# Routed FFN's weights in runs of 2 KB, two weight tiles in other buffers, and the output bias as a row of the projection

## The chip, the cores and the metric

The kernel runs on one core of a Trainium2 chip (trn2). The metric is the device time of one execution in microseconds, median of several runs. A profile is one execution more, with its own time.

## The reference, cut to what matters

For four sequences of 512 tokens with 256 features:

```python
x = x + attn(cond(x, cond_8))          # attention output projection: ... @ Wo.T + bo
x = x + ffn(cond2(x, cond_8))          # routed FFN of 8 experts, 1024 wide
# ffn: 8 groups of 256 tokens; softmax router, two experts per token, at most 128 rows
# per expert and group
expert_in = jnp.einsum('gth,gtec->gech', xg, dispatch)
h = jax.nn.gelu(jnp.einsum('gech,ehf->gecf', expert_in, wi))
expert_out = jnp.einsum('gecf,efh->gech', h, wo)
out = jnp.einsum('gech,gtec->gth', expert_out, combine)
```

`cond` is a gated FFN with weights chosen per sequence, `cond2` a linear layer whose weights are mixed per sequence. Everything is float32. `attn` has 16 heads of 16 with one shared key and value head.

## The kernel before

**Attention stage** (to about 478 us). The attention of the four sequences runs as 64 steps of a loop written out by hand, 16 steps for each sequence. Each step has score matmuls with their maxima (`maxima`), the same scores with exponentials (`exponentials`), and the product with the values (`weigh`). Beside each step, a table (`beside`, `last`) puts pieces of work of the sequences before and after it: `queries`, `keys`, `values` of the next one, and normalising, output projection (`out0` to `out3`, line 442), mixing (`mix0`, `mix1`), routing and scattering of the earlier ones. [...]

The output projection multiplies `attn` (128 rows: four heads of 32 rows, of which 16 are used) by `wo_sb`. Row 16 of each head holds the softmax sum, so after normalising it is one; the projection's matrix has zeros there. The result has the input x added (line 447) into `r`, which is stored as rows of the output by SP (line 448). The input for this sum is loaded by `residual(b)` (lines 290 to 295): SP loads x in 512 KB into a buffer of one copy, and POOL adds the output bias `bo_sb` to it (line 294). `residual` is called for sequences 0, 1 and 2 at steps 17, 33 and 49 and for sequence 3 after the loop.

**Routing.** A token's features, number, expert and two probabilities form a row of 260 floats. POOL scatters each sequence's rows with eight indirect DMAs (`send`, line 604) into `xp` in HBM, sorted by expert.

**Routed FFN.** The rows are worked on in 39 tiles of 128 rows of one expert (`NTILE`). For a tile t:

- `fetch_in(t)` reads the expert from a table into a register of SP and loads `wi`, 1 MB, 8 KB in one run for each of 128 partitions (line 803);
- `fetch_rows(t)` loads the tile's 128 rows from `xp` (line 815); that of tile 0 and that of tile 5 wait for all scatters issued so far;
- `fetch_out(t)` loads `wo`, 1 MB in the same way (line 824);
- `turn(t)` transposes the rows on PE (line 830), DVE copies the result to SBUF (`xT`, line 832);
- `up(t)` is 32 matmuls (line 849), with the gelu on ACT (line 853);
- `put(t)` is 16 matmuls (line 865), and on DVE a few small instructions for weights (`w0`, `w1`) and row numbers (`at`, four buffers) and the weighting into `y` (line 883). POOL then adds `y` to the output's rows with an accumulating indirect DMA (line 884).

Each accumulating DMA, an add in short, waits for the one before it, since they may meet in the same rows. `wi` and `wo` have three buffers each in the pool `wexp`, `y` has two.

The first five tiles are early ones (`NEARLY`): they are full of rows before the last sequence is routed. `table_of_early`, at step 62, issues `wi` of tiles 0 to 2, the rows of tiles 0 to 4 and `wo` of tiles 0 to 2. The halves of `up` of the early tiles are put between the last sequence's pieces by the list `final`. `table_of_rest` then computes the table of the other 34 tiles, and this follows:

```python
for t in range(NEARLY, NEARLY + 3):
    fetch_in(t)
for t in range(NEARLY):
    put(t)
    if t + 3 < NEARLY:
        fetch_out(t + 3)
```

After it, the loop over the other 34 tiles has `up(t)`, `fetch_in(t + 3)`, `fetch_rows(t + 3)`, `turn(t + 1)`, `put(t - 1)` and `fetch_out(t + 2)` in this order.

All plain loads and stores stand in one queue, SP's; scatters and adds stand in POOL's.

Of the kernel before, what the change touches and what calls it, by code (L numbers as in the profile page):

```python
# [9 lines left out]
F32 = mybir.dt.float32  # L10
I32 = mybir.dt.int32
AF = mybir.ActivationFunctionType
ALU = mybir.AluOpType
# [3 lines left out]
P = 128  # L17
B = 4
T = 512
NT = B * T  # L20
D = 256
NE = 8
HC = 512
NH = 16
HD = 16
F = 1024
# [5 lines left out]
NTILE = 2 * NCH + NE - 1  # L32
NEARLY = 5
# [5 lines left out]
def adaln_attn_ffn_kernel(  # L39
# [10 lines left out]
    wv: bass.AP,  # L50
    bv: bass.AP,
    wo: bass.AP,
    bo: bass.AP,
    xtok: bass.AP,
    w2: bass.AP,
    mask2: bass.AP,
# [6 lines left out]
    nc = tc.nc  # L63
# [3 lines left out]
    wexp = ctx.enter_context(tc.tile_pool(name="wexp", bufs=3))  # L67
# [47 lines left out]
    qp = attn_ctx.enter_context(tc.tile_pool(name="qp", bufs=2))  # L115
# [29 lines left out]
    def load(ap, shape, name):  # L145
        t = const.tile(shape, F32, name=name)
        nc.sync.dma_start(t, ap)
        return t
# [5 lines left out]
    wv_sb = load(wv, [P, 2, 32], "wv_sb")  # L154
    bv_sb = load(bv[0:1, :].to_broadcast([P, 32]), [P, 32], "bv_sb")
    wo_sb = load(wo, [P, 4, D], "wo_sb")
    bo_sb = load(bo[0:1, :].to_broadcast([P, D]), [P, D], "bo_sb")
    bias2_sb = load(bias2[0:1, :].to_broadcast([P, D]), [P, D], "bias2_sb")
    wr_sb = load(wr, [P, 2, NE], "wr_sb")

# [129 lines left out]
    def residual(b):  # L290

        t = rp.tile([P, 4, D], F32, name="x", bufs=1)
        nc.sync.dma_start(t, xtok[:, ts(b, 4), :])
        nc.gpsimd.tensor_tensor(t, t, bo_sb.unsqueeze(1).to_broadcast([P, 4, D]), ALU.add)
        seqs[b]["x"] = t

    def project(b):
# [444 lines left out]
    def experts_of_tiles(t0, n, end, step, start):  # L742


        past = fp.tile([P, n, NE], F32, name=f"past{t0}", bufs=1)
        nc.vector.tensor_tensor(
            past, tilen[:, 0:n].unsqueeze(2).to_broadcast([P, n, NE]),
            end.unsqueeze(1).to_broadcast([P, n, NE]), ALU.is_ge,
        )
        te = texp[:, t0 : t0 + n]  # L750
        nc.vector.tensor_reduce(te, past, AX.X, ALU.add)
        nc.vector.tensor_scalar(
            table[:, 1, t0 : t0 + n], te, float(NE - 1), float(P), ALU.min, ALU.mult
        )
        nc.vector.tensor_tensor(past, past, step.unsqueeze(1).to_broadcast([P, n, NE]), ALU.mult)
        row = fp.tile([P, n], F32, name=f"trow{t0}", bufs=1)
        nc.vector.tensor_reduce(row, past, AX.X, ALU.add)
        if start is not None:
            nc.vector.tensor_scalar(row, row, start, None, ALU.add)
        nc.vector.tensor_tensor(row, row, tilen[:, 0:n], ALU.add)  # L760
        nc.vector.tensor_scalar(
            table[:, 0, t0 : t0 + n], row, float(NE * NG), float(P), ALU.min, ALU.mult
        )

    def table_of_early():
        tiles_of_experts(full, -float(P), ALU.is_ge)
        end = ends_of_experts(full, "end0")
        step = fp.tile([P, NE], F32, name="step0", bufs=1)
        nc.vector.tensor_scalar(step, full, -1.0, float(NG), ALU.mult, ALU.add)
        experts_of_tiles(0, NEARLY, end, step, None)  # L770

        nc.vector.tensor_tensor(used[:, 0:NE], full, end, ALU.subtract)
        nc.vector.tensor_scalar(
            used[:, 0:NE], used[:, 0:NE], float(NEARLY), 0.0, ALU.add, ALU.max
        )
        nc.vector.tensor_tensor(used[:, 0:NE], used[:, 0:NE], full, ALU.min)
        for t in range(3):
            fetch_in(t)
        for t in range(NEARLY):
            fetch_rows(t)  # L780
        for t in range(3):
            fetch_out(t)

    def table_of_rest():
        tiles = fp.tile([P, NE], F32, name="tiles", bufs=1)
# [10 lines left out]
    reg, adds, spare = {}, [], {}  # L796
    AFTER = mybir.DependencyInfo(mybir.DependencyClass.Sync, mybir.DependencyReason.DATA)

    def fetch_in(t):

        reg[t] = nc.sync.value_load(table[0:1, 1, t : t + 1], min_val=0, max_val=(NE - 1) * P)
        wi_of[t] = wexp.tile([P, 2, F], F32, name="wi_sb")
        nc.sync.dma_start(wi_of[t].rearrange("p c f -> p (c f)"), wi[ds(reg[t], P), :])

    def fetch_rows(t):

# [13 lines left out]
            tc.add_to_no_dep_group("early tiles", i.ins)  # L820

    def fetch_out(t):
        wo_of[t] = wexp.tile([P, F // P, D], F32, name="wo2_sb")
        nc.sync.dma_start(wo_of[t].rearrange("p c f -> p (c f)"), wo2[ds(reg.pop(t), P), :])

    def turn(t):

# [30 lines left out]
    def put(t, halves=(0, 1)):  # L858

        if halves[0] == 0:  # L860
            po_of[t] = bank("e")
        po = po_of[t]
        for half in halves:
            for fc in range(4 * half, 4 * half + 4):
                mm(  # L865
                    po[:, 0:D], hT_of[t][:, fc, :], wo_of[t][:, fc, :],
                    start=fc == 0, stop=fc == F // P - 1,
                )
        if halves[-1] == 0:
            return  # L870
        xt = xt_of[t]
        number, e0, p0, p1 = (xt[:, D + k : D + k + 1] for k in range(4))
        te = texp[:, t : t + 1]
        w0 = fp.tile([P, 1], F32, name="w0")
        nc.vector.tensor_scalar(w0, e0, te, p0, ALU.is_equal, ALU.mult)  # L875
        w1 = fp.tile([P, 1], F32, name="w1")
        nc.vector.tensor_scalar(w1, e0, te, p1, ALU.not_equal, ALU.mult)  # L877
        nc.vector.tensor_tensor(w0, w0, w1, ALU.add)
        nc.vector.tensor_scalar(w1, number, 0.0, spare1, ALU.is_equal, ALU.mult)
        at = fp.tile([P, 1], I32, name="at", bufs=4)  # L880
        nc.vector.scalar_tensor_tensor(at, number, -1.0, w1, ALU.add, ALU.add)
        y = fp.tile([P, D], F32, name="y")
        nc.vector.tensor_scalar(y, po[:, 0:D], w0, None, ALU.mult)  # L883
        i = nc.gpsimd.indirect_dma_start(  # L884
            out=out_rows,
            out_offset=bass.IndirectOffsetOnAxis(ap=at, axis=0),
            in_=y,
            in_offset=None,
            compute_op=ALU.add,
        )  # L890

        if t > 0:
            tc.add_manual_dep(i.ins, adds[-1].ins.name, AFTER, reason="same rows")
        if t < NEARLY:
            tc.declare_no_dep(i.ins, group="last rows", reason="other sequences")
            tc.add_to_no_dep_group("early adds", i.ins)
        if t == NEARLY:
            for k in last_rows:
                tc.add_manual_dep(i.ins, k.ins.name, AFTER, reason="rows of the last sequence")
        adds.append(i)  # L900

    for n in range(STEPS + 1):
        m = n + LEAD
        if n % 16 == 1 and n > 1:
            residual(n // 16 - 1)
        if m < STEPS:
            maxima(m, (0, 1))
            exponentials(n, (2, 3))
        elif n < STEPS:
            exponentials(n, (0, 1, 2, 3))  # L910
        if n > 0:
            weigh(n - 1)
        if m < STEPS:
            maxima(m, (2, 3))
            exponentials(n, (0, 1))
        if m <= STEPS + 1 and m % 4 == 1:
            shifted(m // 4 - 1)
        if n < STEPS:
            side(*divmod(n, 16))
    work[B - 1] = finish(B - 1)  # L920
    residual(B - 1)
    def half_up(t, half):
        if half == 0:
            turn(t)
# [16 lines left out]
        fetch_in(t)  # L941
    for t in range(NEARLY):
        put(t)
        if t + 3 < NEARLY:
            fetch_out(t + 3)
        if t == 2:
            for k in range(NEARLY, NEARLY + 3):
                fetch_rows(k)
            fetch_out(NEARLY)
        if t == 3:  # L950
            fetch_out(NEARLY + 1)
    turn(NEARLY)
    for t in range(NEARLY, NTILE + 1):
        if t < NTILE:
            up(t, (0, 1))
            if t + 3 < NTILE:
                fetch_in(t + 3)
                fetch_rows(t + 3)
            if t + 1 < NTILE:
                turn(t + 1)  # L960
        if t > NEARLY:
            put(t - 1)
        if t + 2 < NTILE:
            fetch_out(t + 2)


def _layouts(i):
# [3 lines left out]
    def halves(w):  # L971

        *lead, k, n = w.shape
        return np.swapaxes(w.reshape(*lead, k // P, P, n), -3, -2)

    i = {name: np.asarray(a) for name, a in i.items()}
    f32 = np.float32
# [19 lines left out]
    bv = np.ones((1, 32), f32)  # L997
    bv[0, :HD] = bkv[HD:]
    wo = np.zeros((4, 32, 4, D), f32)
    wo[:, :HD] = i["L0_attn_Wo"].T.reshape(4, 4, HD, D).transpose(1, 2, 0, 3)  # L1000
    bias2 = i["L0_cond2_bias"]
    return {
# [8 lines left out]
        "wv": wv,  # L1011
        "bv": bv,
        "wo": wo.reshape(P, 4, D),
        "bo": i["L0_attn_bo"].reshape(1, D),
        "xtok": i["x"].reshape(NCH, P, D).transpose(1, 0, 2),
        "w2": halves(np.swapaxes(i["L0_cond2_weight"], 1, 2)).transpose(1, 0, 2, 3),
        "mask2": halves(i["L0_cond2_mask"].T),
        "bias2": bias2.reshape(1, D),
        "wr": halves(i["L0_ffn_w_router"]),
        "wi": halves(i["L0_ffn_wi"]).reshape(NE * P, 2 * F),  # L1020
        "wo2": halves(i["L0_ffn_wo"]).reshape(NE * P, F * D // P),
    }


# [21 lines left out]
```

## Time and profile before

| | |
|---|---|
| runs (us) | 836.52, 837.17, 837.45; median 837.17 |
| profiled execution | 838.61 us, span from first to last instruction 836.9 |
| busy in the span | PE 768.9 us (92%), PE weight loads 483.6, DVE 351.0, ACT 246.8, POOL 126.8 |
| DMA | 122.21 MB, 146 GB/s on the mean |
| mean granted PE clock | 0.959 |

The span counts from the first to the last instruction; the execution's own time is 1.7 us longer. A line of the timeline or of the groups names the engine (PE matmul, PEld weight load, DVE, ACT, POOL; SPq is SP's queue of DMA issues), the line of the kernel, the operation, and the tiles written and read. Buffer numbers are left out of names, so `wo_sb` is both the attention's projection and the FFN's second weights, `x` both the input and the rows to be scattered. The brackets at the end of a timeline row say how long the engine stood idle before it and what ended that.

### The profile page before, as it was taken

The numbers are of one execution on the slowest core, as the hardware profiler recorded it, in microseconds if no ns is written. First come the engines' busy times: TensorE is split into PE (matmuls) and PEld (weight loads), VectorE is DVE, ScalarE is ACT, GpSimd is POOL, SyncE is SP. The second block draws the span as 40 slices with busy tenths as digits, with TensorE's granted clock in tenths as the row PEclk, the third lists the DMA queues.
The fourth block names the chain that finished last, engine by engine and source line by source line (L and its number), as shares of the span: only waits on it lengthen the run. The fifth ranks groups of instructions, "written<-read, shape, count | busy, mean of one in ns | idle before, by whom it ended". The sixth has DMA issues, their size and how long they took to land. (4 is left out here: it accounts for less than half of the span.)

```text
span 836.9 us, 11311 instructions
## 1 busy us (share of the span) xinstructions
PE 768.9 (92%) x4382; PEld 483.6 (58%) x4382; DVE 351.0 (42%) x826; ACT 246.8 (29%) x419; POOL 126.8 (15%) x128
## 2 busy tenths in 40 slices
PE   2999999999999999999899777948999999999994
PEld 1443433333345434545254266837999989999994
DVE  0165454556655567646875431431222222212221
ACT  0112206554643555434335510301111111111110
POOL 6400010000000010120103301042211212212222
PEclk9999999999999999989899959978999999999998
DMA  8993000000000100020001273196999999999972
GB/s 311 317 296 79 1 25 1 1 1 1 0 1 20 33 0 1 15 88 1 1 14 64 81 287 118 51 339 185 361 304 339 316 320 319 330 296 344 318 239 25
DMA packets 40389, 122.21 MB, mean 146 GB/s; under 512 B 4624, under 2 KB 25360, under 8 KB 29840
## 3 DMA queue, kind: packets, MB, share of 16 engines
q1 hardware_dynamic: 32032, 105.81, 36.3%
q0 software_dynamic: 8304, 15.69, 7.6%
q8 instruction: 34, 0.56, 0.3%
q14 instruction: 19, 0.16, 0.1%
HBM read 101.36 MB, written 20.12 MB: 145 GB/s over the span
## 5 line engine op out<-in xcount | busy, mean ns | idle before, releaser
L353 DVE TENSOR_REDUCE negm<-ps_m 128x1 f32<-128x512 f32 x250 | 160.7, 686 | 103.6 <-PE ps_e L379 95.3
L380 ACT ACTIVATE e<-ps_e 128x512 f32<-128x512 f32 x244 | 132.6, 595 | 152.4 <-PE ps_e L379 141.4
L379 PE MATMUL ps_e<-qs,k 32*128 32x512 f32 x488 | 158.1, 656 | 1.8 <-DVE sm L516 0.9
L849 PE MATMUL ps_m<-xT,wi_sb 128*128 128x128 f32 x1248 | 150.4, 279 | 8.9 <-DVE xT L832 8.3
L349 PE MATMUL ps_m<-k,q 32*128 32x512 f32 x500 | 153.5, 652 | 2.8 <-DVE negm L353 2.7
L849 PEld LDWEIGHTS ps_m<-xT,wi_sb 128*128 128x128 f32 x1248 | 147.9, 195 | 13.8 <-DVE xT L832 11.5
L865 PE MATMUL ps_e<-wo_sb,hT 128*128 128x256 f32 x560 | 126.5, 379 | 0.0
L853 ACT ACTIVATE hT<-ps_m 128x512 f32<-128x512 f32 x70 | 41.8, 597 | 241.6 <-PE ps_m L849 226.8
L865 PEld LDWEIGHTS ps_e<-wo_sb,hT 128*128 128x128 f32 x560 | 103.8, 190 | 12.7
L349 PEld LDWEIGHTS ps_m<-k,q 32*128 32x128 f32 x500 | 42.8, 186 | 87.8 <-DVE negm L353 44.8
L884 POOL DMA_INDIRECT out_dram<-y,at x39 | 60.5, 1551 | 216.0 <-DVE y L883 185.5
L883 DVE TENSOR_SCALAR y<-ps_e,w 128x256 f32<-128x256 f32 x39 | 18.9, 484 | 169.7 <-DMA out_dram<-y,at 146.0
L391 PE MATMUL ps_a<-e,v 128*32 128x512 f32 x512 | 69.8, 618 | 1.1 <-ACT e L380 1.1
L379 PEld LDWEIGHTS ps_e<-qs,k 32*128 32x128 f32 x488 | 52.1, 186 | 10.8 <-ACT e L380 10.2
L604 POOL DMA_INDIRECT xp<-x,to_i x32 | 31.6, 987 | 103.6 <-issue 47.3
L260 PE MATMUL ps_a<-xT_sb,wi_sb 128*128 128x512 f32 x64 | 32.3, 629 | 15.7 <-DMA wi_sb<-in_wcond_dram,rows 15.7
L536 POOL TENSOR_SCALAR x<-mk 128x4 f32<-128x4 f32 x4 | 0.8, 198 | 261.9 <-DVE mk L533 261.9
L391 PEld LDWEIGHTS ps_a<-e,v 128*32 128x32 f32 x512 | 10.2, 109 | 51.7 <-issue 47.3
L307 PE MATMUL ps_c<-coT,wq_sb 128*128 128x512 f32 x64 | 34.5, 671 | 2.0 <-ACT q L308 2.0
L442 PE MATMUL ps_c<-wo_sb,attn 128*128 128x256 f32 x128 | 31.9, 402 | 4.1 <-DVE r L447 4.1
L832 DVE COPY xT<-ps_a 128x256 f32<-128x256 f32 x39 | 16.3, 417 | 44.5 <-PE ps_a L830 44.5
L265 DVE SCALAR_TENSOR_TENSOR hid<-ps_e,wo_sb,sg 128x512 f32<-128x512 f32 x16 | 12.0, 750 | 51.5 <-PE ps_e L262 50.2
(155 smaller groups left out, 631.7 us busy)
## 6 DMA issues: line engine op xcount, KB each, us to landing
wi_sb<-in_wi_dram SPq DMA_DIRECT2D x39, 1024.0 KB
wo_sb<-in_wo_dram SPq DMA_DIRECT2D x39, 1024.0 KB
xp<-zeros SPq DMA_DIRECT2D x1, 8450.0 KB
xt<-xp SPq DMA_DIRECT2D x34, 130.0 KB
xT_sb<-in_xT_dram SPq DMA_DIRECT2D x4, 512.0 KB
w_sb<-in_w_dram SPq DMA_DIRECT2D x8, 256.0 KB
x<-in_xtok_dram SPq DMA_DIRECT2D x4, 512.0 KB
out_dram<-r SPq DMA_DIRECT2D x16, 128.0 KB
```

The costliest lines, as they stand in the source:

```text
L260: mm(pu, wu[:, c, ts(hc, P)], xT_sb[:, c, ts(b, T)], start=c == 0, stop=c == 1)
L307: mm(pq, wq_sb[:, c, i, :], coT[:, c, ts(b, T)], start=c == 0, stop=c == 1)
L349: mm(pm, q[32 * j : 32 * j + 32, ds((4 * hg + hh) * P, P)], k[32 * j : 32 * j + 32, :], start=True, stop=True,)
L353: nc.vector.tensor_reduce(nm[:, hh, j, HD : HD + 1], pm, AX.X, ALU.max, negate=True)
L379: mm(px, k[rows_j, ts(sc, P)], qs_of[u][rows_j, :], start=True, stop=True)
L380: nc.scalar.activation(e_of[n][:, :, j, :], px.rearrange("p (h n) -> p h n", h=4), AF.Exp)
L391: mm(pa_of[u][32 * hh : 32 * hh + 32, :], seqs[b]["v"][:, sc, :], e[:, hh].rearrange("p j n -> p (j n)"), start=sc == 0, stop=sc == 3,)
L442: mm(px[:, 0:D], s["attn"][:, hg, ts(ch, P)], wo_sb[:, hg, :], start=hg == 0, stop=hg == 3,)
L849: mm(ph[:, ts(n, P)], wi_of[t][:, c, ts(4 * half + n, P)], xT_of[t][:, c, :], start=c == 0, stop=c == 1,)
L853: nc.scalar.activation(hT_of[t][:, ds(4 * half, 4), :].rearrange("p f t -> p (f t)"), ph, AF.Gelu_apprx_tanh,)
L865: mm(po[:, 0:D], hT_of[t][:, fc, :], wo_of[t][:, fc, :], start=fc == 0, stop=fc == F // P - 1,)
L884: i = nc.gpsimd.indirect_dma_start(out=out_rows, out_offset=bass.IndirectOffsetOnAxis(ap=at, axis=0), in_=y, in_offset=None, compute_op=AL ...
```

## The change

Four things change.

1. **Runs of 2 KB.** `wi` and `wo` of each expert lie in HBM as four blocks of 256 KB, each with 2 KB for every partition, so a tile's load has four runs of 2 KB for each partition instead of one of 8 KB. The SBUF side is as before.
2. **Buffers.** `wo` of tile 3 goes into a buffer of the pool that holds the queries (`q`), `wo` of tile 4 into one that holds attention output (`o`), both of 8 KB for each partition and out of use by then. Both are issued in `table_of_early`. In the loop over `put` of the early tiles, `wo` of tiles 5 and 6 is then issued before the rows of tiles 5 to 7, and `wo` of tile 7 after them. `y` of tiles 0 to 3 lies in the place of the buffer `rT`; from tile 4 on `y` has three buffers.
3. **Bias.** The output bias is the projection matrix's row 16 of the first head, where the attention has its one. The load of `bo_sb` and POOL's additions are gone.
4. **x** is loaded at steps 0, 28, 44 and 57.

```diff
@@ residual
         t = rp.tile([P, 4, D], F32, name="x", bufs=1)
         nc.sync.dma_start(t, xtok[:, ts(b, 4), :])
-        nc.gpsimd.tensor_tensor(t, t, bo_sb.unsqueeze(1).to_broadcast([P, 4, D]), ALU.add)
@@ experts_of_tiles
-            table[:, 1, t0 : t0 + n], te, float(NE - 1), float(P), ALU.min, ALU.mult
+            table[:, 1, t0 : t0 + n], te, float(NE - 1), 4.0 * P, ALU.min, ALU.mult
@@ table_of_early
         for t in range(3):
             fetch_out(t)
+        for t in range(3, NEARLY):
+            expert_of(t)
+            fetch_out(t)
@@
+    def expert_of(t):
+        reg[t] = nc.sync.value_load(table[0:1, 1, t : t + 1], min_val=0, max_val=(NE - 1) * 4 * P)
+
+    def quarters(w, src, row):
+        nc.sync.dma_start(
+            w.rearrange("p a b -> p (a b)").rearrange("p (q n) -> p q n", q=4),
+            src[ds(row, 4 * P), :].rearrange("(q p) n -> p q n", p=P),
+        )
+
     def fetch_in(t):
-        reg[t] = nc.sync.value_load(table[0:1, 1, t : t + 1], min_val=0, max_val=(NE - 1) * P)
+        if t not in reg:
+            expert_of(t)
         wi_of[t] = wexp.tile([P, 2, F], F32, name="wi_sb")
-        nc.sync.dma_start(wi_of[t].rearrange("p c f -> p (c f)"), wi[ds(reg[t], P), :])
+        quarters(wi_of[t], wi, reg[t])
     def fetch_out(t):
-        wo_of[t] = wexp.tile([P, F // P, D], F32, name="wo2_sb")
-        nc.sync.dma_start(wo_of[t].rearrange("p c f -> p (c f)"), wo2[ds(reg.pop(t), P), :])
+        if t == NEARLY - 2:
+            w = qp.tile([P, T, 4], F32, name="q").rearrange("p (f a) i -> p f (a i)", f=F // P)
+        elif t == NEARLY - 1:
+            w = ep.tile([P, 4, 512], F32, name="o").rearrange("p g (a d) -> p (g a) d", a=2)
+        else:
+            w = wexp.tile([P, F // P, D], F32, name="wo2_sb")
+        quarters(w, wo2, reg[t])
+        wo_of[t] = w
@@ put
-        y = fp.tile([P, D], F32, name="y")
+        if t < 4:
+            if t == 0:
+                spare["y"] = rp.tile([P, 2, T], F32, name="rT", bufs=1).rearrange(
+                    "p a (b d) -> p (a b) d", d=D
+                )
+            y = spare["y"][:, t, :]
+        else:
+            y = fp.tile([P, D], F32, name="y", bufs=3)
@@ the steps
-        if n % 16 == 1 and n > 1:
-            residual(n // 16 - 1)
+        if n in (0, 28, 44, 57):
+            residual((0, 28, 44, 57).index(n))
@@
     work[B - 1] = finish(B - 1)
-    residual(B - 1)
@@ the early tiles
     for t in range(NEARLY):
         put(t)
-        if t + 3 < NEARLY:
-            fetch_out(t + 3)
-        if t == 2:
+        if t < 3:
+            fetch_out(NEARLY + t)
+        if t == 1:
             for k in range(NEARLY, NEARLY + 3):
                 fetch_rows(k)
-            fetch_out(NEARLY)
-        if t == 3:
-            fetch_out(NEARLY + 1)
@@ the other tiles
-        if t + 2 < NTILE:
+        if NEARLY + 3 <= t + 2 < NTILE:
             fetch_out(t + 2)
@@ layouts on the host
+    def quarters(w):
+        return np.swapaxes(halves(w).reshape(NE, P, 4, 512), 1, 2).reshape(-1, 512)
...
+    wo[0, HD, 0] = i["L0_attn_bo"]
...
-        "wi": halves(i["L0_ffn_wi"]).reshape(NE * P, 2 * F),
-        "wo2": halves(i["L0_ffn_wo"]).reshape(NE * P, F * D // P),
+        "wi": quarters(i["L0_ffn_wi"]),
+        "wo2": quarters(i["L0_ffn_wo"]),
```

More of the change, by code (lines that the diff above doesn't have):

```diff
@@ L52, in adaln_attn_ffn_kernel @@
     wo: bass.AP,
-    bo: bass.AP,
     xtok: bass.AP,
@@ L156, in adaln_attn_ffn_kernel @@
     wo_sb = load(wo, [P, 4, D], "wo_sb")
-    bo_sb = load(bo[0:1, :].to_broadcast([P, D]), [P, D], "bo_sb")
     bias2_sb = load(bias2[0:1, :].to_broadcast([P, D]), [P, D], "bias2_sb")
@@ L1013, in _layouts @@
         "wo": wo.reshape(P, 4, D),
-        "bo": i["L0_attn_bo"].reshape(1, D),
         "xtok": i["x"].reshape(NCH, P, D).transpose(1, 0, 2),
```

## The prediction

> **What bounds the kernel now.** I read the page's busy rows first (PE 92% of the span), then who waited for whom on PE, then the timeline where PE waits, then the chain that ended last, and last the packet records behind the DMA rows.
>
> PE's waits (us in total, times, longest):
>
> ```profile
> PE ps_e L865 <- DMA wo_sb<-in_wo_dram: 10.4, 1, 10.4
> PE ps_m L849 <- DVE xT L832: 8.3, 9, 2.7
> PE ps_c L442 <- DVE r L447: 4.1, 1, 4.1
> ```
>
> Single waits, so they have places. The timeline (start, duration) has the first at the change from the five early tiles to the other 34, for PE and then SP's queue:
>
> ```profile
> 547.87 3.72 PE L865 MATMUL ps_e<-wo_sb,e 128*128 128x256 f32 x16 [0.20 <-issue]
> 561.95 6.33 PE L865 MATMUL ps_e<-wo_sb,e 128*128 128x256 f32 x16 [10.36 <-DMA wo_sb<-in_wo_dram]
> 568.11 3.62 PE L865 MATMUL ps_e<-wo_sb,hT 128*128 128x256 f32 x16
> 571.56 0.38 PE L830 MATMUL ps_a<-ident,xt 128*128 128x128 f32 x2
> 574.66 5.19 PE L849 MATMUL ps_m<-xT,wi_sb 128*128 128x128 f32 x32 [2.72 <-DVE xT L832]
> ```
>
> ```profile
> 545.77 5.72 SPq L803 DMA_DIRECT2D wi_sb<-in_wi_dram  x3
> 552.94 2.83 SPq L824 DMA_DIRECT2D wo_sb<-in_wo_dram  x2
> 559.30 2.56 SPq L815 DMA_DIRECT2D xt<-xp  x3
> ```
>
> Tile 3's wo is issued at 552.94, behind wi of tiles 5 to 7, so PE stands 10.36 us. Then up(5) waits 2.72 us for its copy, which DVE has queued behind a y that waits for an add. The other place is the last sequence's output projection:
>
> ```profile
> 501.49 3.62 PE L442 MATMUL ps_c<-wo_sb,attn 128*128 128x256 f32 x16
> 506.34 2.34 POOL L294 TENSOR_TENSOR x<-x,bo_sb 128x1024 f32<-128x1024 f32 x1 [23.04 <-DMA x<-in_xtok_dram]
> ...
> 509.19 1.19 PE L442 MATMUL ps_c<-wo_sb,attn 128*128 128x256 f32 x2 [4.09 <-DVE r L447]
> ```
>
> In the steady stage PE is full, yet the chain runs through the adds to the output:
>
> ```profile
> 648.10 0.50 DVE y L883
> 648.75 8.63 DMA out_dram<-y,at
> 657.47 0.49 DVE y L883
> 657.97 0.16 issue
> 658.13 7.49 DMA out_dram<-y,at
> ```
>
> Each add waits for the one before. From add 7 (issued 603.39) to add 31 (792.69) they came every 189.3/24 = 7.9 us; the last five, beside little weight traffic, every 4.5. PE's own period is 7.245 (SP's wi issues at 627.92, 635.17, 642.41). So **PE and the adds bind together**: y has two buffers, and when adds lag DVE stands in y with the next xT copy behind it. Wi issues from 584.46 to 797.42 span 29 tiles in 212.96 us; 29 x 7.245 is 210.1, so 2.85 us are lost there.
>
> [...] in the 12th us 45 gather packets of 8 KB ran beside 42 plain ones of 2 KB. [...] 8 KB takes 309 ns, 2 KB 84 (medians), four of which are 336, 8.7% dearer. [...] The granted clock was 0.60 from 551.6 to 562, and up(5) took 5.19 us against the steady 3.57.
>
> **Part by part.**
>
> *Bias as a row, x at other steps.* The matmuls keep their shapes (the row was zero), so PE pays nothing. One 128 KB load and four POOL adds of 2.34 us go; only the last of these was waited for. x of the last sequence now stands at step 57, ahead of all expert weights on SP; its buffer is free once sequence 2's r is written (440.5), 34 us before SP's next work (475.38). Those of the sequences before move to steps 0, 28 and 44, each still behind the stores of the sequence ahead of it and with nothing urgent behind it on SP: no cost. The wait of 4.1 goes, and the slow clock after it (the next 16 matmuls took 5.41, not 3.62: 1.8): **5.9 us**. Next late is r itself, 0.4 us after its matmuls, which PE already shows.
>
> *wo of tiles 3 and 4 in q and o.* Their slots are free by step 59 (last reader of q) and 52. SP does two register loads (1.1 us each) and two DMAs more before wi(3), at about 494 to 500; wo(0) to wo(4) are 5.2 MB, landed by about 510 at the rate of that stage, and needed from 534.7. wi(3) comes after them, about 511, needed at 526. PE then runs put(0) to put(4) in one piece: put(2) ended at 551.6, now 545.7, plus 2 x 3.46: PE is ready at 552.6. Next late are tile 5's rows. The last scatter's issue ended at 553.1 and SP's wait for it at 559.2; now 547.2 and about 553. But xt(5) lies in the ring behind wi(5..7), wo(5), wo(6): 5 x 32 packets x 84 ns = 13.4 us, and eight scatters x 2 x 161 ns = 2.6, from 546.7 - 5.9 = 540.8: 556.8. Landing 1 us, transpose and copy 0.9: **up(5) at 558.7** instead of 574.66. PE idles 6 us again, so up(5) stays slow (-0.3). Gain to here 15.7, the 5.9 included. Bounds: rows there in time give up(5) at 553.5 (5.2 more); rows landing at 561, 3.2 less. wo(5) and wo(6) wait for put(0) and put(1), by then done, and wo(7) is issued after the rows, 15 us before its use.
>
> *y: four in rT's place, then three buffers.* y(4) waits for nothing, so xT(5) isn't held. In the steady stage y(t) waits for add(t-3). `at` keeps four buffers; at(4) waits for add(0), landed by 556 (9 us after 547, as before), before xT(5) can start anyway.
>
> *2 KB runs.* A tile's packets per engine, at medians: before 16 x 309 + 8 x 47 (xt) + 8 x 102 (add) = 6.14 us of 7.245. After: 64 x 84 + 1.19 = **6.57 us**. The DMA share of 0.96 (600 to 680 us) counts overlapping packets twice and is no objection. PE stays the bound while a 2 KB packet costs under (7245 - 1192)/64 = 94.6 ns. Rows for it: 85.1 mean from 10 to 27 us beside gathers, 102.5 mean (median 84) at 5 to 9.4 us, alone, on xT. I take 86. SP's issue grows: two 2 KB pieces a partition took 0.6 us there against 0.33 for one, so I take 1.2 for four, 3 us of SP's 7.245 a tile, beside PE.
>
> The adds: unloaded, first packet 2.1 us after issue, packets over 1.3, next issue 1.1 later: 4.5. Loaded 3.4, 2.6 and 1.25 (means). Each add packet now waits for one of 84 ns instead of 309: 8 x 0.225 = 1.8 less; so about 5.5, bounds 4.5 and 7.9. Below 7.245 y never waits and the **2.85 us** come back; the tail after the last put is the same two adds.
>
> Sum: 15.7 + 2.85 = 18.5. The profiled execution took 838.61 (span 836.9 and 1.7 around it), so 820.1; the median of the runs is 1.4 lower, 837.17: **819**.
>
> **Rivals.**
> - *Rows there in time* (no wait at 552.6): 21.2 + 1.6 (clock) + 2.85 = 25.6, so 812. Against it: five weight tiles lie ahead of xt(5). 0.06.
> - *Adds stay at 7.9.* They then set the end: add 5 comes at about 579 instead of 588.9 and the rest follow as before, 7 to 10 us gained (the quiet stretch at the end may be shorter): 827 to 830. For it: first-packet delay may not shrink with packet size. 0.10.
> - *SP late*: at 546 to 556 SP's steps took 0.7 us each; if five issues of four pieces take 2.8 us each, rows come 8 to 10 us later: 826 to 829. 0.08.
> - *2 KB packets at 94.6 to 102.7 ns*: DMA binds by up to 0.52 a tile x 34 = 17.6: 822 to 837. 0.08, of which 0.02 within 0.2% of before.
> - *Slower: DMA becomes the bound outright.* The four quarters of a tile are 256 KB apart in HBM[...]; from 102.7 ns on, just over the dearer row above, the gain is eaten: 34 x (64 x 102.7 + 1192 - 7245) ns = 17.7. At 110 ns a tile takes 8.23, +33.6 - 18.5 = +15: 852. For it: the only stage with 2 KB runs alone had that mean. Against: its median was 84, its slow packets all lie in the first 9 us, and beside gathers the same size ran at 85. 0.10.
> - That wo(3), wo(4) move without coming earlier can't be: SP's order in the changed program has them before wi(3).
>
> **How the numbers follow.** Likeliest 0.58: 819, own range 814.5 to 824. The range 812 to 831 holds nearly all of that, half of the first rival, most of the adds and SP cases, half of the dear-packet case: 0.79. A difference of 0.2% (1.7 us) is about what a measurement tells from no change. Faster 0.88 (0.58 + 0.06 + 0.10 + 0.08 + 0.06), same 0.02, slower 0.10.
>
> **What would show it.** Right: no wait of PE for r at L442's successor; put(0) to put(4) back to back; up(5) near 559 with xt(5) its releaser; wi issues 7.245 apart; add intervals under 7 with the chain on PE; 2 KB packets near 86 ns. Wrong: steady wi issues over 7.3 apart with PE waiting for wi_sb or wo_sb (DMA bound); a chain still of adds end to end (rival two); up(5) after 563 (SP or scatters).

## The result, and the profile after

The changed kernel takes 824.81 us (median of 823.81, 824.65, 824.97 and 828.15), the kernel before 837.31 us beside it: ratio 0.985, 95% interval 0.981 to 0.989. In a second set of runs beside other runs of before, it was 0.982 (0.977 to 0.987). The forecast was 819, range 812 to 831. The profiled execution took 823.81, 14.8 less than the 838.61 of before.

The page of the changed kernel: span, PE's row, and the shares of the chain that ended last.

```profile
span 822.1 us, 11304 instructions
PE 759.0 (92%) x4382; PEld 479.7 (58%) x4382; DVE 349.4 (43%) x826; ACT 246.8 (30%) x419; POOL 116.9 (14%) x124
PE 28%; DMA 4%; issue 1%; POOL 0%; POOLq 0%; DVE 0%; SPq 0%
```

PE's waits for DMA and DVE around the experts (total, times, longest), then PE's timeline at the change from the early tiles to the rest, and SP's queue there:

```profile
PE ps_a L848 <- DMA xt<-xp: 5.6, 1, 5.6
PE ps_m L867 <- DVE xT L850: 4.4, 6, 1.8
```

```profile
496.04 7.07 PE L440 MATMUL ps_c<-wo_sb,attn 128*128 128x256 f32 x32
...
539.93 3.62 PE L883 MATMUL ps_e<-q,e 128*128 128x256 f32 x16
545.11 3.69 PE L883 MATMUL ps_e<-o,hT 128*128 128x256 f32 x16 [1.57 <-issue]
554.41 0.66 PE L848 MATMUL ps_a<-ident,xt 128*128 128x128 f32 x2 [5.61 <-DMA xt<-xp]
```

```profile
542.95 1.46 SPq L804 DMA_DIRECT2D wo_sb<-in_wo_dram  x2
547.14 2.58 SPq L826 DMA_DIRECT2D xt<-xp  x3
```

The two single waits of before are gone: the projection of the last sequence (first row) runs through, and tile 3's wo (now in `q`) is there. One gap of 1.57 us is left ahead of tile 4's `put`. What is late next is tile 5's rows, as forecast: they are issued at 547.14 behind five weight tiles and PE stands 5.61 us for them. `up(5)` starts at 555.59 instead of 574.66. From 577.2 to 787.3 SP issues wo in 29 periods of 7.245 us: PE is full. The chain's share of PE, 28%, is mostly this stretch; its 4% of DMA are the adds below, and tile 5's rows with the scatters ahead of them.

The end is another matter. Last pieces of the chain that ended last (start, duration, what), and the last rows of the timeline for the last y and the last add:

```profile
789.09 0.49 DVE y L908
...
789.73 4.53 DMA out_dram<-y,at
...
795.01 3.76 DMA out_dram<-y,at
...
799.53 3.85 DMA out_dram<-y,at
```

```profile
805.05 0.48 DVE L908 TENSOR_SCALAR y<-ps_e,w 128x256 f32<-128x256 f32 x1 [1.97 <-PE ps_e L883]
808.69 1.54 POOL L909 DMA_INDIRECT out_dram<-y,at  x1 [3.03 <-DMA out_dram<-y,at]
813.21 1.54 POOL L909 DMA_INDIRECT out_dram<-y,at  x1 [2.98 <-DMA out_dram<-y,at]
```

The last five adds run end to end, and the last is issued 8.16 us after the last y; before it was 1.95. The adds still came 182.9/24 = 7.62 us apart (from add 7 to add 31), where 5.5 was forecast and PE needs 7.245. So they fell behind PE in the steady stage, and what PE had gained was partly given back at the end.

Because the clock's slow stretches fall differently in each execution (last section), the runs below are held against each other by distances within one trace, from the first y (tile 0) on. Before took 829.55, 830.28 and 834.76 us beside the three groups of experiments, while their expectations in us were written beside 837: for times, the ratios count. The profiled execution of two loads, 828.97 us, was the slowest of its six.

| kernel | first y at | first to last y | first y to last add | add interval, 7 to 28 |
|---|---|---|---|---|
| before | 547.33 | 278.7 | 280.7 | 7.88 |
| after | 535.84 | 269.2 | 277.4 | 7.72 |
| after, again | 534.40 | 269.4 | 278.4 | 7.85 |
| 8 KB runs | 522.56 | 271.1 | 277.5 | 7.96 |
| y as before | 532.17 | 276.0 | 278.2 | 7.55 |
| wo as before | 523.82 | 273.7 | 281.1 | 7.79 |
| x's steps as before | 543.10 | 269.2 | 277.6 | 7.61 |
| bias and x as before | 541.09 | 270.9 | 280.5 | 7.68 |
| few weights | 524.93 | 269.7 | 271.2 | (PE's 7.25 once caught up) |
| four loads | 524.38 | 269.5 | 271.4 | 7.23 |
| two loads | 543.02 | 272.0 | 274.5 | 7.47 |
| four loads, rows first | 529.80 | 263.0 | 265.6 | 7.07 |
| four loads, rows earlier | 535.13 | 267.2 | 269.3 | 7.28 |

The gain of the profiled execution follows from two columns: the first y is 547.33 - 535.84 = 11.5 earlier, and the last add 280.7 - 277.4 = 3.3 nearer to it; 838.6 - 11.5 - 3.3 = 823.8. PE's own part after the first y, 278.7 - 269.2 = 9.5, appears in neither.

Of the two, the 3.3 is fairly steady (the second trace of the changed kernel has 278.4; of before there is one). The 11.5 is a difference of two executions and can't be taken for the worth of the change: in the eleven traces with bias and x as in the changed kernel, the first y runs from 522.56 to 543.02. Two things move it. One is half clock, 10.2 to 44.4 us ahead of the first y; at the same 44.4 us, two loads is only 547.33 - 543.02 = 4.3 us ahead of before. The other is ACT, which stands 4.7 to 7.6 us ahead of its last copy into `o`, between 473 and 483 us, in six traces (before, the changed kernel twice, two loads, by partitions, rows earlier) and 1.2 us in the other eight; no run shows why. What holds is the medians: the whole gain is 12.5 us in the first set of runs and 14.7 in the second.

### The profile page after: what moved, and what is told of

The parts are those of the page before. It is cut to its first block, busy times and chain, and to the rows that moved or that the text cites. A ratio compares the mean times of both kernels' runs of the same rounds, so it can differ in the third digit from the quotient of the medians.

```text
span 822.1 us, 11304 instructions
## 1 busy us (share of the span) xinstructions
PE 759.0 (92%) x4382; PEld 479.7 (58%) x4382; DVE 349.4 (43%) x826; ACT 246.8 (30%) x419; POOL 116.9 (14%) x124
## 5 line engine op out<-in xcount | busy, mean ns | idle before, releaser
L377 PE MATMUL ps_e<-qs,k 32*128 32x512 f32 x488 | 156.0, 646 | 2.5 <-ACT e L378 1.1
L347 PE MATMUL ps_m<-k,q 32*128 32x512 f32 x500 | 151.0, 644 | 0.6 <-DVE negm L351 0.5
L883 PE MATMUL ps_e<-wo_sb,hT 128*128 128x256 f32 x544 | 122.9, 379 | 0.0
L883 PEld LDWEIGHTS ps_e<-wo_sb,hT 128*128 128x128 f32 x544 | 100.8, 190 | 12.3
L909 POOL DMA_INDIRECT out_dram<-y,at x35 | 53.8, 1538 | 197.4 <-DVE y L908 129.0
L908 DVE TENSOR_SCALAR y<-ps_e,w 128x256 f32<-128x256 f32 x35 | 16.9, 484 | 128.0 <-DMA out_dram<-y,at 72.6
L377 PEld LDWEIGHTS ps_e<-qs,k 32*128 32x128 f32 x488 | 52.2, 185 | 11.5 <-ACT e L378 10.9
L389 PEld LDWEIGHTS ps_a<-e,v 128*32 128x32 f32 x512 | 10.2, 109 | 50.6 <-issue 46.3
L261 PE MATMUL ps_e<-xT_sb,wi_sb 128*128 128x512 f32 x64 | 31.3, 612 | 0.0
```

The source lines that it names most:

```text
L347: mm(pm, q[32 * j : 32 * j + 32, ds((4 * hg + hh) * P, P)], k[32 * j : 32 * j + 32, :], start=True, stop=True,)
L377: mm(px, k[rows_j, ts(sc, P)], qs_of[u][rows_j, :], start=True, stop=True)
L389: mm(pa_of[u][32 * hh : 32 * hh + 32, :], seqs[b]["v"][:, sc, :], e[:, hh].rearrange("p j n -> p (j n)"), start=sc == 0, stop=sc == 3,)
L883: mm(po[:, 0:D], hT_of[t][:, fc, :], wo_of[t][:, fc, :], start=fc == 0, stop=fc == F // P - 1,)
L909: i = nc.gpsimd.indirect_dma_start(out=out_rows, out_offset=bass.IndirectOffsetOnAxis(ap=at, axis=0), in_=y, in_offset=None, compute_op=AL ...
```

## What was won before the first expert

The forecast gave 5.9 us to the wait for x. A second cost of the bias showed only when the two timelines were laid side by side, although its wait stands in the list of PE's waits of before:

```profile
PE ps_m L349 <- DVE negm L353: 2.7, 1, 2.7
```

Before, POOL and DVE near 401 us, and PE behind them:

```profile
399.60 0.19 DVE L532 TENSOR_TENSOR eq<-eq,rev 128x32 f32<-128x32 f32 x1
...
400.93 2.33 POOL L294 TENSOR_TENSOR x<-x,bo_sb 128x1024 f32<-128x1024 f32 x1
400.94 2.37 DVE L532 TENSOR_TENSOR eq<-eq,rev 128x32 f32<-128x32 f32 x1
...
404.42 1.22 PE L349 MATMUL ps_m<-k,q 32*128 32x512 f32 x1 [2.73 <-DVE negm L353]
```

The same operation of DVE takes 0.19 us, and 2.37 when POOL's addition of the bias has started 0.01 us ahead of it. PE waits 2.73 us behind it and its clock is half from 403.45 to 410.28. The changed kernel has no such addition, and its row is short:

```profile
400.05 0.19 DVE L530 TENSOR_TENSOR eq<-eq,rev 128x32 f32<-128x32 f32 x1
```

Before, POOL's addition takes 2.33 us and DVE's operation 2.37, and they end 0.05 us apart (403.26 and 403.31). Not every operation of DVE is held so: three maxima (`negm<-ps_m`, line 353) that ran beside POOL's addition at 305.61 in the same trace took 0.68 to 0.69 us, and their mean over the span is 0.686. What decides it, no run shows.

**Bias and x's steps as before**, the rest as changed:

```diff
...
+        nc.gpsimd.tensor_tensor(t, t, bo_sb.unsqueeze(1).to_broadcast([P, 4, D]), ALU.add)
...
-        if n in (0, 28, 44, 57):
-            residual((0, 28, 44, 57).index(n))
+        if n % 16 == 1 and n > 1:
+            residual(n // 16 - 1)
...
+    residual(B - 1)
-    wo[0, HD, 0] = i["L0_attn_bo"]
```

> The changed kernel with POOL's addition of the bias and x's steps as before. Theory (POOL's additions, by their hold on DVE and by the wait of the last, cost what the profiles differ by before the first y, 547.33 - 535.84 = 11.5 us): DVE's long operation near 401 us and PE's waits of some 2.7 and 4.1 us are back; 8 to 12 us above the changed kernel's, ratio 0.995 to 0.999. Rival (of the 11.5 only the 5.9 of the prediction belong to the bias and x; the rest was where the clock's slow stretches happened to fall in that execution): ratio 0.990 to 0.993.

Measured: ratio 1.000 (0.998 to 1.002). Its timeline has the hold again:

```profile
390.32 2.33 POOL L294 TENSOR_TENSOR x<-x,bo_sb 128x1024 f32<-128x1024 f32 x1
390.33 2.37 DVE L532 TENSOR_TENSOR eq<-eq,rev 128x32 f32<-128x32 f32 x1
...
393.81 0.69 PE L349 MATMUL ps_m<-k,q 32*128 32x512 f32 x1 [2.73 <-DVE negm L353]
```

The rival's 0.990 to 0.993 lies outside the interval; the theory's 0.995 to 0.999 was a little low. By the time, without this part nothing is left of 1.5%. But PE's wait for r is 11.9 us here, not 4.1, so 7.8 us of that wait are a cost that the rest of the change makes. What bias and x alone would bring to the kernel before was not run.

**x's steps alone as before**: the second and third hunk above, bias still a row.

> The changed kernel with x loaded at the steps of before (17, 33, 49 and after the loop), bias still a row of the projection. Theory (half of what was won ahead of the experts came from POOL's addition going, which at 400.9 us held [...]an operation of DVE that took 2.37 us instead of 0.19, PE behind it 2.73 us, and its clock was half for 6.8 us after): that stays won; at the output projection of the last sequence PE waits at most 4.1 - 2.3 = 1.8 us for x, or nothing: time 0 to 3 us above the changed kernel's, ratio 0.984 to 0.989. Rival (the steps of the loads are what counts): 6 us or more back, ratio 0.992 or higher.

Measured: 824.6 us against 830.28, ratio 0.994 (0.992 to 0.997). The rival's number came (0.992 or higher), but both expectations missed the reason. SP's queue and PE:

```profile
488.15 1.39 SPq L804 DMA_DIRECT2D o<-in_wo_dram  x1
...
489.54 3.62 PE L440 MATMUL ps_c<-wo_sb,attn 128*128 128x256 f32 x16
489.58 3.07 SPq L292 DMA_DIRECT2D x<-in_xtok_dram  x1
...
503.84 6.53 PE L440 MATMUL ps_c<-wo_sb,attn 128*128 128x256 f32 x16 [10.69 <-DVE r L445]
```

With wo of tiles 3 and 4 issued early (tile 3's into `q` just before the rows shown, tile 4's into `o`), x at its old place stands behind 2 MB more, and PE waits 10.69 us for r. So loading x at step 57 doesn't only take away the old 4.1; it is the condition under which the two wo can come early. Between these two runs lies POOL's addition alone: (1.000 - 0.994) x 830, about 5 us (the medians differ by 7.7), and the intervals don't meet. PE's 2.73 is seen in the trace. That the rest is slow clock after it, as in before, is not shown: these two traces have 27.3 us of half clock ahead of the first y with the addition, and 37.5 without.

## Where the experts' gain went

**8 KB runs**: `quarters` and its host layout undone, one run a partition.

```diff
-            w.rearrange("p a b -> p (a b)").rearrange("p (q n) -> p q n", q=4),
-            src[ds(row, 4 * P), :].rearrange("(q p) n -> p q n", p=P),
+            w.rearrange("p a b -> p (a b)"), src[ds(row, P), :]
...
```

> The changed kernel with its weights in runs of 8 KB again; buffers, bias row and x steps as changed. Theory A (the four 2 KB runs of a partition take one turn of a DMA engine together, so that finer runs brought the adds next to nothing; and the adds, one after another, set the end): add intervals of 7.6 to 7.9 us as in either kernel, PE's steady period 7.245 still, and with up to 0.27 us more for each of some 26 adds 824 to 832 us, most likely 827. Rival B (runs of 2 KB are what makes the adds quicker): intervals over 8, end 7 us or more later, 832 to 838. Rival C (2 KB runs are a loss, 336 ns for 8 KB against 309): weights land sooner, xt of tile 5 about 1 us earlier, 820 to 824.

Measured: 813.21 us against 829.55, ratio 0.983 (0.980 to 0.987), within the interval of the changed kernel. 277.5 us from first y to last add, as with 2 KB. A finer packet brings neither the adds nor the time anything that can be measured. That the four runs take one turn of an engine is the author's guess; no run shows it. Only PE differs, in one trace: from tile 8 on it took 7.373 us a tile, now and then waiting for xT (up to 1.2 us), where the changed kernel has 7.245; the adds at the end hid it.

**y as before**: two buffers.

```diff
-        if t < 4:
...
-            y = fp.tile([P, D], F32, name="y", bufs=3)
+        y = fp.tile([P, D], F32, name="y")
```

> The changed kernel with y in two buffers for every tile, none in rT's place. Theory A (the adds run end to end from the third tile on, 7.6 us each beside the weights, and set the end): y(4) stands on DVE for add 2 and holds up the copy xT of tile 5, so up(5) starts 5 to 8 us later than 555.6, PE loses about 3 us more in the steady stage, DVE's wait for adds doubles from 72.6 us; yet the adds are not later by more than 1 us, and the time stays within 2 us of 824.8: 823 to 827. Rival (the end is PE's last put and a few adds after it, as predicted): the time rises by what PE loses, 8 to 11 us, to 832 to 836.

Measured: ratio 0.985 (0.981 to 0.990). PE's longest wait for xT is 7.0 us, and the last y comes 276.0 us after the first instead of 269.2; the last add only 278.2 instead of 277.4. So PE loses 6.8 us and the end 0.8: theory A. Two numbers of it were wrong. DVE's waits for adds fell to 41.6 us where they should have doubled. And PE lost all of its 6.8 us ahead of tile 5 (`up(5)` comes 26.6 us after the first y instead of 19.7); the 3 us more in the steady stage didn't come, where it ran at 7.245 with two buffers too.

**wo as before**: tiles 3 and 4 in the weights' pool, after `put(0)` and `put(1)`.

```diff
-        for t in range(3, NEARLY):
-            expert_of(t)
-            fetch_out(t)
...
-        if t < 3:
-            fetch_out(NEARLY + t)
-        if t == 1:
+        if t + 3 < NEARLY:
+            fetch_out(t + 3)
+        if t == 2:
             for k in range(NEARLY, NEARLY + 3):
                 fetch_rows(k)
...
```

> The changed kernel with wo of tiles 3 and 4 in the weights' own pool again, issued after put(0) and put(1), and the rows of tiles 5 to 7 after put(2), as in the kernel before; 2 KB runs, y's buffers, bias row and x steps as changed. Theory (the adds, 7.7 us each beside the weights and started by put(0), set the end, so that PE's earlier up(5) is mostly given back): PE waits some 10 us for wo again, the last y comes 7 to 10 us later after the first y than the changed kernel's 269.2 us, but the last add only 0 to 4 us later than its 277.4: time 0 to 4 us above the changed kernel's, a ratio to before of 0.985 to 0.990. Rival (PE sets the end, as predicted: this part is worth 9.8 us): ratio 0.995 to 0.998.

Measured: ratio 0.986 (0.982 to 0.990). PE's wait is back:

```profile
PE ps_e L875 <- DMA wo_sb<-in_wo_dram: 11.6, 1, 11.6
```

An 11.6 us wait of PE costs 273.7 - 269.2 = 4.5 us at the last y, less than the 7 to 10 of the theory, and 281.1 - 277.4 = 3.7 at the last add, inside what it allowed; the rival's ratio lies outside the interval. In the time, the two early wo bring nothing that can be measured.

**Few weights**: tiles 13 to 38 load none.

```diff
+        if t > 12:
+            wi_of[t] = wi_of[12]
+            return
...
+        if t > 12:
+            wo_of[t] = wo_of[12]
+            return
```

> The changed kernel, but the tiles after the 13th use the weights of the 13th again: the loads of wi and wo of tiles 13 to 38 are left out (so those tiles are computed with another expert's weights); PE's work, the rows and the adds stay. Theory (weight packets slow the adds, and the adds set the end): from there on adds take 4.5 us each, the backlog is gone by about tile 20, the last add is issued about 0.7 us after the last y and the time is 7 us below that of the changed kernel, 816 to 819 (PE loses nothing). Rival (the adds are slow for a reason of their own, such as rows written twice or POOL's descriptors): intervals stay at 7 or more and the time at 823 to 826.

Measured: ratio 0.977 (0.972 to 0.981). Adds 5 to 7, beside weights, were 7.1 to 8.0 us apart; adds 9 and 10, after the last weights, 4.5; from add 12 on each follows its y at PE's 7.25, with its packets through 3.5 us after issue. The last add comes 271.2 us after the first y, 6.2 less, while the last y stays where it was (269.7). The adds' pace is set by the weight traffic, and it cost the changed kernel some 6 us. The distances show this; the time's interval meets that of the changed kernel's second set.

## How the weights are cut

The forecast's packet argument had one loose end: in the changed kernel, scatters moved 31 packets beside 136 weight packets of 2 KB in a microsecond, not one for one; before, 32 beside 38 of 8 KB (from 541 and from 554 us). From these numbers comes the author's guess that an engine takes the four runs of a partition as one turn.

**Four loads** of one run a partition:

```diff
-        nc.sync.dma_start(
-            w.rearrange("p a b -> p (a b)").rearrange("p (q n) -> p q n", q=4),
-            src[ds(row, 4 * P), :].rearrange("(q p) n -> p q n", p=P),
-        )
+        flat = w.rearrange("p a b -> p (a b)")
+        for q in range(4):
+            nc.sync.dma_start(flat[:, ts(q, 512)], src[ds(row + q * P, P), :])
```

> The changed kernel with each weight tile fetched by four loads of one 2 KB run a partition instead of one load of four runs a partition; the same bytes in the same packets. Theory A (an engine serves the four runs of one partition in one turn, and an add's packet waits 4 x 84 ns for it): now a packet of an add waits for one of 84 ns, the add interval falls from 7.6 to about 5.5 to 6, the adds catch up with PE, the end follows the last put by 5 to 10 us instead of 12, and the time is 815 to 819, unless SP, which then issues eight loads a tile, comes late (PE would wait for wi_sb or wo_sb). Rival (the adds are slow because the engines are full, whatever the order of turns): intervals 7.4 to 7.9, time 823 to 828.

Measured: 806.63 us against 829.55, ratio 0.975 (0.971 to 0.979). End of its chain:

```profile
786.93 3.47 PE ps_e L882 x16
...
790.42 0.50 DVE y L907
...
791.18 3.85 DMA out_dram<-y,at
```

Ahead of the last add the chain waits for one add, not five, and everything before that is PE. Y never waits for an add in the steady stage. The 815 to 819 of theory A, written beside 837, are 0.973 to 0.978, and that came, though the interval still meets that of the changed kernel's second set (0.977 to 0.987); the distances tell them apart. The theory's reason fell all the same: scatters still moved 32 packets beside 132 of the weights, and an add takes about 7 us, not 5.5. What differs in the records is the stretch that an add's packets take: 2.5 to 2.7 us on the mean (adds 7 to 27) in the three traces with four loads by columns, 2.9 to 3.3 in before and the others with the full weights on one or two loads. The delay to the first packet is 3.2 to 3.7 us in all of these.

This trace alone doesn't show that the adds keep pace, for it wins its 6 us early: add 5 goes out 35.4 us after the first y, 41.2 in the changed kernel, and from there to the last add both take 236 us. The run with the rows first, below, shows it: there the adds start with a backlog and come 7.07 us apart, less than PE's 7.245.

**Two loads** and **four loads by partitions** were to separate the order of the runs from the size of the portions:

```diff
...
+        to = w.rearrange("p a b -> p (a b)").rearrange("p (q n) -> p q n", q=4)
+        for q in range(0, 4, 2):
+            nc.sync.dma_start(
+                to[:, ds(q, 2)],
+                src[ds(row, 4 * P), :].rearrange("(q p) n -> p q n", p=P)[:, ds(q, 2)],
+            )
```

```diff
...
+        for j in range(4):
+            nc.sync.dma_start(
+                to[ts(j, 32)],
+                src[ds(row, 4 * P), :].rearrange("(q p) n -> p q n", p=P)[ts(j, 32)],
+            )
```

> The changed kernel with each weight tile in two loads by columns, two 2 KB runs a partition in each. If the number of runs of one partition in a row is what slows the adds, this lies between one load and four: adds 7.3 to 7.5 us apart, 273 to 275 us from the first y to the last add, ratio 0.977 to 0.981. If the portions count, the same is expected, so this run tells the size of the effect and not its cause. If neither counts and four loads gained by something else (SP's own delay of the next loads), 277 us and 0.984.

Measured: adds 7.47 us apart, 274.5 us to the last add: between one load and four, as said. The time, 0.981 (0.977 to 0.986), can't be told from one load.

> The changed kernel with each weight tile in four loads, but cut by partitions: each load has 32 partitions with their four 2 KB runs, in the order of the changed kernel. Theory (four issues one after another hand the weights out in smaller portions, and adds find gaps between them, whatever lies in one load): adds take 7.2 us or less and the last add comes 271 to 272 us after the first y, as with four loads by columns, ratio 0.973 to 0.978. Rival (what counts is that the four runs of one partition no longer follow one another): adds 7.6 to 7.8 us apart, 277 us, ratio 0.983 to 0.986, or worse if 32 partitions at a time load more slowly.

Measured: 919 us against 835, a tenth slower, with adds 10.7 us apart and 381.1 us to the last add: the rival's "worse", and no answer to the question, for now the loads themselves are slow. PE's waits, and a window of the steady stage (length; busy time of PE, weight load, DVE, ACT, POOL; granted clock, DMA share, GB/s):

```profile
PE ps_a L850 <- DMA xt<-xp: 82.5, 29, 16.0
```

```profile
600.00:780.00 180.00, 143.37 (x843) 128.62 (x842) 30.18 (x118) 20.30 (x34) 25.19 (x17) 0.89 1.08 221
```

The same 2 KB packets take 153 ns on the mean (600 to 700 us) against 94 to 97 in the changed kernel. SP, too, stands 136 us until earlier pieces of wi and wo have landed, which with four loads by columns is 3.6. This is how the forecast's slower rival looks: PE waits for rows in 29 tiles, and its clock falls to 0.89. The changed kernel has PE busy for all of this window. Why smaller columns help the adds stays open: portions and order were not separated.

**Rows first.** With four loads the start matters again: PE waited 7.7 us for tile 5's rows.

```diff
-        if t < 3:
-            fetch_out(NEARLY + t)
-        if t == 1:
+        if t == 0:
             for k in range(NEARLY, NEARLY + 3):
                 fetch_rows(k)
+        if t < 3:
+            fetch_out(NEARLY + t)
```

> The changed kernel with four loads for each weight tile (as in the run with four loads, 0.975 of before) and the rows of tiles 5 to 7 issued ahead of wo of tiles 5 and 6. Theory (with four loads the adds take 6.9 us, less than PE's 7.245, so that what PE gains early is kept): xt of tile 5 lands 4 to 6 us earlier, PE's wait for it falls from 7.7 to 2 or 3 us, the last y and the last add come 3 to 6 us earlier: ratio 0.968 to 0.972. Rival (the adds have no such room, and the backlog at the start stays to the end): the last y comes earlier, the last add doesn't, ratio 0.974 to 0.977.

Measured: ratio 0.971 (0.966 to 0.976); last y and last add are 6.5 and 5.8 us nearer to the first y than with four loads alone. PE at tile 5:

```profile
543.06 0.41 PE L847 MATMUL ps_a<-ident,xt 128*128 128x128 f32 x2 [2.10 <-DMA xt<-xp]
```

The trace bears the theory out; the times alone (0.971 and 0.975) don't separate the two. Against the changed kernel the intervals don't meet, and this is the lowest ratio found.

**Rows earlier still**, ahead of wi of tiles 6 and 7, against the version with the rows first:

```diff
-    for t in range(NEARLY, NEARLY + 3):
-        fetch_in(t)
+    fetch_in(NEARLY)
     for t in range(NEARLY):
         put(t)
         if t == 0:
             for k in range(NEARLY, NEARLY + 3):
                 fetch_rows(k)
+            fetch_in(NEARLY + 1)
+        if t == 1:
+            fetch_in(NEARLY + 2)
```

> Four loads for each weight tile, and the rows of tiles 5 to 7 directly behind wi of tile 5, ahead of wi of tiles 6 and 7 too. Theory (the scatters and the rows then share the engines with one weight tile, not three): the rows land 2 us or more earlier than with the rows behind all three, PE's wait of 2.1 us for them goes, the last y comes some 261 us after the first, the last add 263 to 266: ratio 0.966 to 0.971. Rival (wi of tile 6 and wo of tile 5 are now late): PE waits for wi_sb or wo_sb for 2 us or more and nothing is gained against the run with the rows first: 0.970 to 0.974.

Measured: 0.979 (0.974 to 0.984). Both expectations missed (0.966 to 0.971, 0.970 to 0.974). Tile 5 no longer waits for rows, but a wait comes up in a place that neither named:

```profile
568.93 0.41 PE L847 MATMUL ps_a<-ident,xt 128*128 128x128 f32 x2 [4.28 <-DMA xt<-xp]
```

That is tile 8. SP now works off wi of two tiles and wo of three after the rows, reaches wi of tile 8 at 560.14 instead of 551.17, and xt of tile 8 behind it. The queue's order moved the wait three tiles on.

**The changed kernel again**, with no edit, beside the last three:

> The changed kernel itself beside the three others, so that they can be held against it on one chip. From the first look: ratio to before 0.981 to 0.989, adds 7.7 us apart, 277 us from the first y to the last add.

Measured: 0.982 (0.977 to 0.987); 278.4 us to the last add.

## Why the prediction was right, and where not

- *Total.* 819 forecast, 824.8 measured, inside the range; of 18.5 us in the profile 14.8 came, but not where they were booked: 5.9 ahead of the first y and 12.6 behind it were forecast, 11.5 and 3.3 came.
- *Bias and x* (5.9): right as to the wait for r, which is gone; short as to "four POOL adds of 2.34 us go; only the last of these was waited for". The one near 401 us held DVE, and PE for 2.73 us. The 5.6 us that came beyond the 5.9 are in part chance: before had 44.4 us of half clock until the first y, after 27.3, and not all of the difference follows a wait: at 365.90 before had 6.83 us of it and after, at 365.81, 3.41, with no wait of PE of 1 us in the 25 us ahead of either.
- *wo early*: back to back, with xt of tile 5 as the releaser and about 6 us of idle PE, as written; PE's clock was half from 553.54 to 560.37, and `up(5)` took 6.10 us. Taken from the first y, `up(5)` is 19.1 - 11.5 = 7.6 us earlier; 15.7 - 5.9 = 9.8 was forecast.
- *y's buffers*: the 2.85 us of the steady stage came back to PE, 7.245 to the last tile, but not for the reason given, "Below 7.245 y never waits": y waited for adds 16 times, 72.6 us in all. Nor do the runs give it to the buffers: with two of them the stage ran at 7.245 too, and with three and 8 KB runs at 7.373 (one trace each). Why it came back stays open.
- *SP*: a load of four runs took 0.37 us to issue, not 1.2; nothing hung on it.
- *2 KB runs*: right that DMA never binds, though its mean of 94 to 97 ns lies over the 86 taken. From 600 to 700 us it was even over the 94.6 at which DMA was to bind (96.6), and PE was busy for all of that time, so the sum of packet times is no limit to go by (packet times overlap: the DMA share of 16 engines reaches 1.08 with four loads by partitions). **The step that failed** is "8 x 0.225 = 1.8 less; so about 5.5": the interval went from 7.89 to 7.62. That each packet of an add waits for one packet of the weights was the author's estimate. The scatters' 31 beside 136 don't bear it out, and beside the weights an add was little quicker: its first packet came 3.5 us after issue and its packets were through in 3.1 (means of adds 7 to 27), before in 3.7 and 3.1. How an engine takes its turns, no run shows. With it fell "the tail after the last put is the same two adds", and 6.2 of PE's 9.5 us came back as adds at the end.
- *Rival "adds stay at 7.9"* is what happened, near enough. Its step, add 5 "at about 579 instead of 588.9", looks good against the measured 577.06, but by luck: counted from the first y, add 5 came at 41.2 us, before at 41.6, so nearly all of it is the gain ahead of the first y. Adds 0 to 4 already ran end to end, so add 5 had almost nothing of the 7.6 us by which `up(5)` was earlier. From there it was 236.1 us to the last add against 239.1.
- *Luck.* The main case came near for a reason that wasn't its own: a larger gain before the experts, in part chance, made up for a loss after them.

Not tried: taking the early wo out of the version with four loads, where the adds leave room and that part may be worth more.

## What to carry to other kernels

When two serial chains run at nearly the same pace (7.245 us a tile and 7.62 an add here), a gain on the engine that the timeline shows waiting can be lost unless the other chain has room: measure the interval of each, and look at what ends after the last matmul. Look for an operation that takes ten times its usual duration (2.37 us for 0.19 here) before you book a removed one at nothing; here the removed addition cost nothing on its own engine, and held its neighbour. A load moved ahead in a queue moves everything behind it back, so ask what stood there: x in one run (10.69 us of PE's time), tile 8's rows in another (4.28).

## What was not expected of the hardware

- In these traces the granted clock falls to half in stretches of 3.413 us or multiples of it (before 3.413, 6.827, 13.653 and 17.067, and 8.820 where the end cuts it off), and not at the same places in each execution. Four loads and rows first are the same program up to the first y; one profile has 13.7 us of half clock there, the other 23.9, and the first y stands at 524.38 and 529.80. The six runs of four loads go from 805.99 (mean clock 0.981) to 814.40 (0.971). Single times under 1% apart say little; distances inside a trace say more.
- A load of 32 partitions with 2 KB runs has packets of 153 ns on the mean; one of 128 partitions with the same runs in the changed kernel, 94 to 97.
- An add without weight traffic beside it has its first packet 2.1 us after its issue and its packets through in 1.0 to 1.5; beside the weights in loads of 128 partitions 3.2 to 3.7 and 2.5 to 3.3, in packets of 2 KB as of 8 KB.
